# Summing half of the GAT batches on VectorE inside PSUM, slot by slot, in place of pairwise sums of slots

## The chip, the core and the metric

The kernel runs on one core of one Trainium2 chip. The metric is the device time of one launch in microseconds (us). The five engines of the core (TensorE or PE for matmuls, VectorE or DVE, ScalarE or ACT, GpSimd or POOL, SyncE or SP) run their own instruction queues in order and meet through semaphores.

## What is computed

Four graph layers run over 2048 nodes with 8 batches of 128 features. The adjacency matrix is sparse (each entry is 1 with chance 1/128), and it is the same for all batches and layers. Layers 0 and 1 are attention layers with a feed-forward part. Layers 2 and 3 are graph attention (GAT) layers, and only these are touched here:

```python
h = x @ W
e = leaky_relu((h @ a_src)[:, :, None] + (h @ a_dst)[:, None, :], 0.2)
e = where(adj == 0, -inf, e)
out = softmax(e) @ h          # per node: a weighted sum of the rows h of its neighbours
y = layer_norm(out + x)
```

## The kernel before

The 2048 nodes are sorted by their number of neighbours and cut into 16 tiles of 128. A tile of 128 nodes needs as many "slots" as its busiest node has neighbours (`CAPS`, 30 down to 11, 277 slots in all). For each slot one indirect DMA (`gather`, line 320), issued by GpSimd, brings the table row of one neighbour for each of the 128 nodes: in a GAT layer 8 batches x 128 values of `h` and 2 x 8 exponentials, 4160 bytes per node. Slots come in chunks of up to four (`pieces`): a GAT layer has 75 chunks, 53 of four slots, 21 of three, and one "folded" chunk of two slots that serves the 16 busiest nodes. Six buffers hold chunks (`bufs`), and gathers are issued up to five chunks ahead (`fetch`).

The program is written out by hand: `layers` walks over the chunks and calls the steps of each chunk (`go`), which are generators. Between the steps `slot` lets the tails of finished tiles advance (`tails`, `threads`). What stands earlier in the program stands earlier in its engine's queue. The framework adds the semaphore waits for every tile that two engines touch.

The steps of one GAT chunk (`gat_chunk`, lines 728 to 776) are:

- Line 745 to 751, DVE: weights of this chunk's slots and batches, into `pair`, which lies in PSUM, and for the last two batches also into `ws` in SBUF.
- Line 757, DVE: batches 0 to 5 of all slots are multiplied by their weights, in place; one operand is in SBUF and one (`pair`) in PSUM. Line 762, ACT: batches 6 and 7 are multiplied by `ws`, one instruction of 128 values for each slot and batch.
- Line 766, DVE: slots are summed in pairs, over all 8 batches: both operands are in SBUF.
- Line 772, PE: the one or two sums that are left are added into `acc`, a PSUM tile of two banks (batches 0 to 3 and 4 to 7), by matmuls with the identity.

The first two steps of chunk c and the last two of chunk c-1 stand in the same turn of the loop, so line 766 of a chunk follows line 757 of the next one. After the last chunk of a tile, `sums` (line 455) and `outputs` (line 649) divide by the weights' sum, and `gat_tail` adds the residual on PE, normalises (`normed`: ACT squares at line 471, `rs` by GpSimd at line 476, ACT scaling at line 480), and in layer 2 projects the result into the next layer's table, which GpSimd writes by an indirect DMA (line 494). In layer 3 it multiplies and adds on DVE (lines 807, 808) and writes the output (line 810). A layer can start in earnest only when the table of the layer before is complete; a few chunks whose neighbours come early are put ahead (`ORDER`, `EARLY`).

Of the kernel before, what the change touches and what calls it, by code (L numbers as in the profile page):

```python
# [17 lines left out]
P = 128  # L18
# [10 lines left out]
NB = 8  # L29
CHUNK = 4 * NB * (D + 2)  # L30
KVB = 6
SCALED = 2


# [48 lines left out]
def sparse_path(ctx: ExitStack, tc: tile.TileContext, ins: dict, out: bass.AP, flag: bass.AP):  # L83
# [19 lines left out]
    def misc():  # L103
        return pm.tile([P, 512], F32, tag="m", name="m")
# [623 lines left out]
    def gat_chunk(l, c):  # L728
        box, t, k, ns = c["box"], c["t"], c["k"], c["ns"]
        mine = own[:, t, :]  # L730
        if c["folded"]:
            pf = misc()[:, :NB]
            nc.tensor.matmul(pf, spread, mine, start=True, stop=True)
            mine = small.tile([P, NB], F32, tag="mine", name="mine", bufs=1)
            nc.scalar.copy(mine, pf)
            yield
        if k == 0:
            box["acc"] = pacc.tile([P, NB // 4, 512], F32, tag="acc", name="acc")
            at, n = (0 if t % 2 == 0 else 512 - NB * CAPS[t]), CAPS[t]
# [5 lines left out]
        nc.vector.tensor_mul(wb, wb, mine[:, None, :].to_broadcast([P, ns, NB]))  # L745
        nc.vector.tensor_max(wc, wa, wb)
        if c["folded"]:
            box["wf"] = small.tile([P, FOLD, NB], F32, tag="wf", name="wf", bufs=1)
            nc.vector.tensor_max(box["wf"], wa, wb)
        ws = small.tile([P, 4, SCALED], F32, tag="ws", name="ws", bufs=3)  # L750
        nc.vector.tensor_max(  # L751
            ws[:, :ns, :], wa[:, :, NB - SCALED :], wb[:, :, NB - SCALED :]
        )
        yield
        hv = hs[:, :, : NB * D].rearrange("p s (b c) -> p s b c", b=NB)
        nv = NB - SCALED
        nc.vector.tensor_mul(  # L757
            hv[:, :, :nv, :], hv[:, :, :nv, :], wc[:, :, :nv, None].to_broadcast([P, ns, nv, D])
        )
        for i in range(ns):  # L760
            for b in range(nv, NB):
                nc.scalar.mul(hv[:, i, b, :], hv[:, i, b, :], ws[:, i, b - nv : b - nv + 1])  # L762
        yield
        left = -(-ns // 2)
        if ns > 1:
            nc.vector.tensor_add(hv[:, : ns - left], hv[:, : ns - left], hv[:, left:ns])  # L766
        yield
        if c["folded"]:
            folded_sums(box["wf"], box)
        for i in range(left):  # L770
            for j in range(NB // 4):
                nc.tensor.matmul(  # L772
                    acc[:, j, :], merge if c["folded"] else ident, hv[:, i, 4 * j : 4 * j + 4, :],
                    start=k + i == 0, stop=c["last"] and i == left - 1,
                )
        yield

    def gat_tail(l, t, box, i):
# [242 lines left out]
    for l in range(4):  # L1021
        per = 2 if l < 2 else 4
        for t, k, ns, folded in pieces(l, per):
# [2 lines left out]
            c["run"] = (attention_chunk if l < 2 else gat_chunk)(l, c)  # L1026
            every.append(c)
    now = [0, 0]

    def advance(group):  # L1030
        for g in list(group):
# [3 lines left out]
    def fetch():  # L1035

        while now[1] < len(every):
            c = every[now[1]]
            l, t, k, ns = c["l"], c["t"], c["k"], c["ns"]

            if now[1] - now[0] > (4 if now[1] >= KVB and every[now[1] - KVB]["l"] > 1 else 3):
                return
            resorted = l > 0 and t < 2 and not c["folded"]
            need = NT - max([b for end, b in EARLY[t] if k + ns <= end] + [0] if resorted else [0])
            if put[l] < need:
                return
            c["buf"] = buffer()[:, : ns * width(l)].rearrange("p (s c) -> p s c", s=ns)
            for i in range(ns):
                at = t * BASE if resorted else first[t]
                index = (sorted_lists if resorted else lists)[:, at + k + i : at + k + i + 1]  # L1050
                gather(l, index, c["buf"][:, i])
            now[1] += 1

    def slot():
        advance(threads)
        advance(tails)
        fetch()

    def drain():
        while threads or tails:  # L1060
# [3 lines left out]
    def later(n, make):  # L1064
        for _ in range(n):
            yield
        yield from make()
# [30 lines left out]
    def layers():  # L1098
        threads.append(find_lists(0))
        state(0, 0)  # L1100
        drain()
        fetch()
        begin(every[0])
        drain()
        threads.append(find_lists(1))
        for i in range(len(every) + 2):
            now[0] = i
            fetch()
            c2, c1, c, n1, n2 = (chunk(i + j) for j in range(-2, 3))
            if c["k"] == 0:  # L1110
                l, t = c["l"], c["t"]
                if l == 0:
                    if t + 2 < NT:
                        threads.append(find_lists(t + 2))
                    if t == 0:
                        state(0, 1)
                        threads.append(later(12, lambda: state(0, 2) or iter(())))
                        threads.append(later(12, clear_late))
                    if t in (2, 6):
                        threads.append(order_lists(t // 4))  # L1120
                while l < 2 and "asked" not in c["box"]:
# [14 lines left out]
            if c1["l"] in (2, 3) and c1["last"]:  # L1136
                sums(c1["l"], c1["t"], c1["box"])
            go(c)
            slot()
            go(c)  # L1140
            slot()
            if c1["l"] in (0, 1) and c1["last"]:
                sums(c1["l"], c1["t"], c1["box"])
            go(c1, 2)
            if c1["l"] in (2, 3) and c1["last"]:
                threads.append(tail(c1["l"], c1["t"], c1["box"]))
            slot()
        verdict()
        drain()
# [529 lines left out]
```

## Time and profile before

| | |
|---|---|
| time | 3421.26 us, median of 3 runs (3419.2 to 3423.05) |
| span in the profile | 3419.3 us |
| busy, share of the span | DVE 90%, PE 80%, POOL 65%, PE weight loads 46%, ACT 42% |
| mean granted clock of TensorE | 0.917 |
| layers 0 and 1 and the preparation | up to about 2235 us |
| first DVE instruction of layer 2; of its folded chunk | 2234.9; 2335.8 us |
| first DVE instruction of layer 3; of its folded chunk | 2799.7; 2877.9 us |
| last DVE sum of slots; end | 3381.5; 3419.3 us |

The landmarks are starts of DVE instructions in the timeline. Between the first instruction of a GAT layer and its folded chunk, seven early chunks run and the core waits for the end of the layer before. The long stretch from the folded chunk on, with the other 67 chunks, is called the main part below: 463.9 us in layer 2 and 503.6 us in layer 3. In the profile, a group's duration is that of one instruction from its start to its last write; instructions that follow each other overlap at their ends, so the distance from start to start in the timeline is what an instruction costs its engine.

### The profile page before, as it was taken

To read this page: it belongs to the slowest core of one execution; us is meant where nothing else is said; L and a number is where in the kernel's file an instruction comes from. 1 tells how busy PE (TensorE), PEld (TensorE's weight loads), DVE (VectorE), ACT (ScalarE), POOL (GpSimd) and SP (SyncE) were. 2 spreads that over 40 slices of the span, in tenths; PEclk is the share of its full clock that TensorE was granted. 3 is DMA by queue.
4 is the path that set the end of the run, shared out by engine and by line. 5 is a ranking of instruction groups with operands and counts; after the bars stand their busy time and mean duration, and the time that the engine had idled before them with its cause. 6 is when DMAs were issued, how large, how long until landed. Compare 5 with 4: busy or idle time off the path is not lost.

```text
span 3419.3 us, 34694 instructions
## 1 busy us (share of the span) xinstructions
PE 2746.3 (80%) x10618; PEld 1585.2 (46%) x10618; DVE 3063.5 (90%) x2727; ACT 1429.0 (42%) x4972; POOL 2213.2 (65%) x1501
## 2 busy tenths in 40 slices
PE   5647888888989997788888999985888976667775
PEld 4523445445555653455545555642444543233332
DVE  7789999999999989999999999965888876788885
ACT  5711333334444541233334344443555654344444
POOL 0065788688667655465676756646788865688873
PEclk9878999999999999999999999987999997889888
DMA  8487877888888777687887887757999986789883
GB/s 340 181 333 266 300 284 282 314 299 291 307 305 311 279 265 285 229 328 282 318 323 291 300 307 277 283 184 267 334 337 349 346 307 241 276 296 319 297 286 123
DMA packets 200881, 986.52 MB, mean 289 GB/s; under 512 B 32174, under 2 KB 33968, under 8 KB 128692
## 3 DMA queue, kind: packets, MB, share of 16 engines
q0 software_dynamic: 175280, 890.45, 71.8%
q1 hardware_dynamic: 20502, 75.52, 5.7%
q10 hardware_dynamic: 4904, 18.24, 1.4%
q8 instruction: 87, 1.43, 0.2%
q14 instruction: 108, 0.88, 0.1%
HBM read 937.16 MB, written 91.55 MB: 301 GB/s over the span
## 4 chain that ended last, share of the span: by engine, by line
DVE 34%; PE 23%; issue 18%; DMA 10%; POOL 6%; ACT 3%; POOLq 0%; DVEq 0%; ACTq 0%
DVE kv L620 12%; DVE kv L606 12%; PE acc L630 7%; PE acc L772 6%; DMA kv<-table,lists 5%; POOL kv L320 4%; DVE sc L609 2%; DVE kv L757 2%; DMA kv<-table,sorted_lists 2%; DVE kv L766 2%; PE m L712 2%; DVE sums L455 1%; DMA table<-rows,perm 1%; PE m L329 1%; PE m L691 1%
## 5 line engine op out<-in xcount | busy, mean ns | idle before, releaser
L320 POOL DMA_INDIRECT kv<-table,lists x955 | 1422.8, 1490 | 352.6 <-issue 205.8
L630 PE MATMUL acc<-kv,ident 128*128 128x512 f32 x2200 | 1107.2, 633 | 229.4 <-DVE kv L620 229.2
L772 PE MATMUL acc<-kv,ident 128*128 128x512 f32 x1184 | 618.2, 672 | 203.0 <-DVE kv L766 155.6
L630 PEld LDWEIGHTS acc<-kv,ident 128*128 128x128 f32 x2200 | 413.9, 202 | 663.1 <-issue 367.5
L606 DVE TENSOR_TENSOR kv<-kv,q 128x2048 f32<-128x2048 f32 (+1 forms) x282 | 629.4, 2232 | 18.9 <-DMA kv<-table,lists 10.1
L609 DVE TENSOR_REDUCE sc<-kv 128x128 f32<-128x2048 f32 (+1 forms) x284 | 634.0, 2233 | 9.2
L620 DVE TENSOR_TENSOR kv<-kv,w 128x2048 f32<-128x2048 f32 (+1 forms) x284 | 631.5, 2224 | 8.2 <-ACT w L615 7.4
L476 POOL TENSOR_TENSOR rs<-ss,half 128x4 f32<-128x4 f32 x192 | 290.5, 1513 | 422.6 <-ACT n L471 421.1
L471 ACT ACTIVATE n<-m,eps 128x128 f32<-128x128 f32 x768 | 271.9, 367 | 568.7 <-PE m L712 216.7
L772 PEld LDWEIGHTS acc<-kv,ident 128*128 128x128 f32 x1184 | 243.4, 216 | 508.2 <-issue 299.4
L757 DVE TENSOR_TENSOR kv<-kv,pair 128x3072 f32<-128x3072 f32 (+1 forms) x150 | 466.3, 3108 | 1.0
L766 DVE TENSOR_TENSOR kv<-kv 128x2048 f32<-128x2048 f32 (+1 forms) x150 | 296.2, 1975 | 147.3 <-ACT kv L762 147.3
L762 ACT ACTIVATE kv<-kv,ws 128x128 f32<-128x128 f32 x1108 | 339.4, 406 | 146.3 <-DVE ws L751 118.9
L480 ACT ACTIVATE n<-m,rs 128x128 f32<-128x128 f32 x768 | 219.6, 370 | 371.5 <-POOL rs L476 371.2
L615 ACT ACTIVATE w<-sc,lmask 128x64 f32<-128x64 f32 x554 | 164.9, 351 | 457.6 <-DVE sc L609 457.0
L320 POOL DMA_INDIRECT kv<-table,sorted_lists x153 | 199.9, 1307 | 114.5 <-PE acc L630 47.6
L494 POOL DMA_INDIRECT table<-rows,perm x57 | 106.5, 1868 | 110.2 <-ACT rows L518 26.4
L329 PE MATMUL m<-ident,n 128*128 128x128 f32 x640 | 106.9, 289 | 85.3 <-ACT n L480 85.3
L471 ACT ACTIVATION_READ_ACCUMULATOR n<-m,eps 128x1 f32 x768 | 157.4, 205 | 0.0
L712 PE MATMUL m<-w_L_w,hT 128*128 128x128 f32 x1024 | 156.4, 275 | 0.0
L329 PEld LDWEIGHTS m<-ident,n 128*128 128x128 f32 x640 | 81.5, 146 | 142.2 <-ACT n L480 92.7
L712 PEld LDWEIGHTS m<-w_L_w,hT 128*128 128x128 f32 x1024 | 135.2, 192 | 0.0
(234 smaller groups left out, 3237.8 us busy)
## 6 DMA issues: line engine op xcount, KB each, us to landing
kept<-xT SPq DMA_DIRECT2D x48, 512.0 KB, 7.6
xT<-kept SPq DMA_DIRECT2D x48, 512.0 KB, 6.4
kv<-in_adj_dram SPq DMA_DIRECT2D x16, 1024.0 KB, 6.4
table<-kv ACTq DMA_DIRECT2D x16, 1024.0 KB, 4.3
kv<-table,lists POOLq DMA_INDIRECT x955, 7.0
kv<-in_x_nodes_dram SPq DMA_DIRECT2D x16, 512.0 KB, 6.6
kv<-table,sorted_lists POOLq DMA_INDIRECT x153, 6.2
found<-cand POOLq DMA_DIRECT2D x16, 64.0 KB, 4.1
```

What stands on the lines that cost most here:

```text
L320: nc.gpsimd.indirect_dma_start(out=dst, out_offset=None, in_=tables[l][:, :], in_offset=bass.IndirectOffsetOnAxis(ap=index, axis=0), bound ...
L471: nc.scalar.activation(dst[:, i, :], z[:, i, :], AF.Square, bias=eps, scale=D**-0.5, accum_out=ss[:, i : i + 1],)
L476: nc.gpsimd.tensor_tensor(rs, ss, half, op=ALU.pow)
L606: nc.vector.tensor_mul(kk, kk, q[:, None].to_broadcast([P, ns, NB, D]))
L609: nc.vector.tensor_reduce(sc[:, :ns].rearrange("p s (b h) -> p (s b) h", h=NH), kk.rearrange("p s b (h j) -> p (s b) h j", h=NH), axis=AX. ...
L620: nc.vector.tensor_mul(vv, vv, w[:, k : k + ns, :].rearrange("p s (b h) -> p (s b) h", h=NH)[:, :, None, :] .to_broadcast([P, ns * NB, HD, ...
L630: nc.tensor.matmul(acc[:, j, :], merge if c["folded"] else ident, kv[:, i, 4 * j : 4 * j + 4, D:], start=k + i == 0, stop=c["last"] and i ...
L712: nc.tensor.matmul(y[:, j, :], hT[:, f, j, :], wt["2"][:, f, :], start=False, stop=f == 1, skip_group_check=True,)
L757: nc.vector.tensor_mul(hv[:, :, :nv, :], hv[:, :, :nv, :], wc[:, :, :nv, None].to_broadcast([P, ns, nv, D]))
L762: nc.scalar.mul(hv[:, i, b, :], hv[:, i, b, :], ws[:, i, b - nv : b - nv + 1])
L766: nc.vector.tensor_add(hv[:, : ns - left], hv[:, : ns - left], hv[:, left:ns])
L772: nc.tensor.matmul(acc[:, j, :], merge if c["folded"] else ident, hv[:, i, 4 * j : 4 * j + 4, :], start=k + i == 0, stop=c["last"] and i = ...
```

## The change

Batches 0 to 3 no longer go through a product in SBUF, a sum of slots and a matmul. For each slot and each of these four batches one DVE instruction multiplies 128 values by the weight and adds them to the first bank of `acc` (the first slot of a tile only multiplies). The product of line 757 covers only batches 4 and 5, the pairwise sum is gone, and the matmuls add every slot's batches 4 to 7 into the second bank. The weights `ws` are now kept in SBUF for all 8 batches. In the folded chunk the old way stays for the products; its first four batches go through a scratch bank and a copy, and are added to `acc` by one DVE instruction (`add`).

It is meant to take the sum of slots off DVE and, with it, DVE's wait for ACT. Two edits go along: `layers` calls the new third step of a GAT chunk in that chunk's own turn, and `slot` lets the tails advance a second time in every third call (`hurry`) while a GAT layer waits for its table or layer 2 is at its last tile.

```diff
+BANK = 4
 SCALED = 2
...
         nc.vector.tensor_max(wc, wa, wb)
+        ws = small.tile([P, 4, NB], F32, tag="ws", name="ws", bufs=3)
+        nc.vector.tensor_max(ws[:, :ns, :], wa, wb)
+        yield
+        hv = hs[:, :, : NB * D].rearrange("p s (b c) -> p s b c", b=NB)
+        lo, hi = (0 if c["folded"] else BANK), NB - SCALED
+        nc.vector.tensor_mul(
+            hv[:, :, lo:hi, :], hv[:, :, lo:hi, :],
+            wc[:, :, lo:hi, None].to_broadcast([P, ns, hi - lo, D]),
+        )
+        for i in range(ns):
+            for b in range(hi, NB):
+                nc.scalar.mul(hv[:, i, b, :], hv[:, i, b, :], ws[:, i, b : b + 1])
+        yield
+        for i in range(0 if c["folded"] else ns):
+            for b in range(BANK):
+                to, of = acc[:, 0, b * D : (b + 1) * D], ws[:, i, b : b + 1]
+                if k + i == 0:
+                    nc.vector.tensor_scalar_mul(to, hv[:, i, b, :], of)
+                else:
+                    nc.vector.scalar_tensor_tensor(
+                        to, hv[:, i, b, :], of, to, op0=ALU.mult, op1=ALU.add
+                    )
+        yield
...
-        left = -(-ns // 2)
-        if ns > 1:
-            nc.vector.tensor_add(hv[:, : ns - left], hv[:, : ns - left], hv[:, left:ns])
-        yield
...
-        for i in range(left):
-            for j in range(NB // 4):
-                nc.tensor.matmul(
-                    acc[:, j, :], merge if c["folded"] else ident, hv[:, i, 4 * j : 4 * j + 4, :],
-                    start=k + i == 0, stop=c["last"] and i == left - 1,
-                )
+        for i in range(ns):
+            nc.tensor.matmul(
+                acc[:, 1, :], merge if c["folded"] else ident, hv[:, i, BANK:, :],
+                start=k + i == 0, stop=c["last"] and i == ns - 1,
+            )
         yield
...
+    def hurry():
+
+        c = every[min(now[0], len(every) - 1)]
+        return c["l"] == 2 and c["t"] == NT - 1 or c["l"] > 1 and put[c["l"]] < NT
+
     def slot():
         advance(threads)
         advance(tails)
         fetch()
+        beat[0] += 1
+        if beat[0] % 3 == 0 and hurry():
+            advance(tails)
...
             go(c)
             slot()
+            if c["l"] in (2, 3):
+                go(c)
```

More of the change, by code (lines that the diff above doesn't have):

```diff
@@ L746, in gat_chunk @@
         nc.vector.tensor_max(wc, wa, wb)
[L747 to L752, printed above, removed]
-        )
+        ws = small.tile([P, 4, NB], F32, tag="ws", name="ws", bufs=3)
+        nc.vector.tensor_max(ws[:, :ns, :], wa, wb)
@@ L754, in gat_chunk @@
         yield
         hv = hs[:, :, : NB * D].rearrange("p s (b c) -> p s b c", b=NB)
-        nv = NB - SCALED
+        lo, hi = (0 if c["folded"] else BANK), NB - SCALED
         nc.vector.tensor_mul(
-            hv[:, :, :nv, :], hv[:, :, :nv, :], wc[:, :, :nv, None].to_broadcast([P, ns, nv, D])
+            hv[:, :, lo:hi, :], hv[:, :, lo:hi, :],
+            wc[:, :, lo:hi, None].to_broadcast([P, ns, hi - lo, D]),
         )
         for i in range(ns):
-            for b in range(nv, NB):
-                nc.scalar.mul(hv[:, i, b, :], hv[:, i, b, :], ws[:, i, b - nv : b - nv + 1])
+            for b in range(hi, NB):
+                nc.scalar.mul(hv[:, i, b, :], hv[:, i, b, :], ws[:, i, b : b + 1])
@@ L767, in gat_chunk @@
         yield
         if c["folded"]:
-            folded_sums(box["wf"], box)
-        for i in range(left):
-            for j in range(NB // 4):
-                nc.tensor.matmul(
-                    acc[:, j, :], merge if c["folded"] else ident, hv[:, i, 4 * j : 4 * j + 4, :],
-                    start=k + i == 0, stop=c["last"] and i == left - 1,
-                )
+            folded_sums(ws, box)
+            pf = misc()
+            for i in range(ns):
+                nc.tensor.matmul(pf, merge, hv[:, i, :BANK, :], start=i == 0, stop=i == ns - 1)
@@ new lines, in gat_chunk, with add @@
+            merged = work.tile([P, 4, P], F32, tag="oT", name="merged")
+            merged = merged.rearrange("p b c -> p (b c)")
+            nc.scalar.copy(merged, pf)
+            def add():
+                nc.vector.tensor_add(acc[:, 0, :], acc[:, 0, :], merged)
+                yield
+            threads.append(later(4, add))
+        for i in range(ns):
[3 more added lines that the diff above has]
+            )
@@ L1028, in sparse_path @@
     now = [0, 0]
+    beat = [0]
     def advance(group):
```

## The prediction

> **What bounds the kernel now.** Only layers 2 and 3 change, so I read those stages: first the busy time by stage, then the waits of DVE there, then DVE and POOL side by side. The table by stage (columns: stretch, length, then busy us and instructions of PE, PEld, DVE, ACT, POOL, granted clock, DMA share, GB/s; the rows from folded chunk to the layer's end are the main parts):
>
> ```profile
> 2234.90:2335.80 100.90, 68.41 (x319) 43.53 (x318) 44.06 (x42) 45.73 (x171) 40.19 (x39) 0.83 0.50 174
> 2335.80:2799.70 463.90, 386.98 (x1454) 217.06 (x1454) 391.97 (x421) 254.24 (x998) 370.07 (x297) 0.93 0.94 339
> 2799.70:2877.90 78.20, 50.83 (x206) 30.15 (x206) 41.92 (x38) 33.03 (x134) 33.14 (x30) 0.83 0.56 202
> 2877.90:3381.50 503.60, 353.22 (x859) 159.55 (x860) 426.73 (x477) 223.78 (x847) 380.88 (x300) 0.86 0.84 289
> ```
>
> No engine is busy all the time: DVE 392 of 464 us and 427 of 504. The waits of DVE over both layers say where its rest goes:
>
> ```profile
> DVE kv L766 <- ACT kv L762: 147.3, 52, 10.0
> DVE kv L745 <- DMA kv<-table,lists: 46.0, 2, 33.5
> DVE kv L745 <- DMA kv<-table,sorted_lists: 26.9, 9, 11.1
> ```
>
> The two DMA lines are the starts of the layers; inside the main parts gathered rows are hardly waited for (2.8 and 2.9 us). So the pairwise sum waits for ACT's products. ACT in turn waits 277.3 us in these layers at line 480 for `rs` on POOL. And POOL? A gather has a gap of 0.30 us behind it, so its engine is taken 370 + about 0.3 x 270, which is nearly the whole 464 us. It should not be: the shortest gather takes 0.99 us, the mean 1.22 to 1.27. The timelines of POOL and DVE at the same moment show why:
>
> ```profile
> 3172.14 0.99 POOL L320 DMA_INDIRECT kv<-table,lists  x1 [0.31 <-issue]
> 3173.44 2.79 POOL L320 DMA_INDIRECT kv<-table,lists  x1 [0.30 <-issue]
> 3176.54 0.99 POOL L320 DMA_INDIRECT kv<-table,lists  x1 [0.30 <-DMA kv<-table,lists]
> ```
>
> ```profile
> 3169.81 3.35 DVE L757 TENSOR_TENSOR kv<-kv,pair 128x3072 f32<-128x3072 f32 x1
> 3173.08 2.29 DVE L766 TENSOR_TENSOR kv<-kv 128x2048 f32<-128x2048 f32 x1
> 3175.28 0.18 DVE L745 TENSOR_TENSOR kv<-kv,own 128x32 f32<-128x32 f32 x1
> ```
>
> The gather that starts during line 766 ends with it (3176.2 against 3175.4); those during line 757 stay at 0.99. So the bound is a loop: the sum blocks POOL, POOL is late with `rs`, ACT is late, and the next sum waits for ACT.
>
> [...] line 757 starts 3.27 us before its successor, 3.20 us of elements plus 0.07, with an operand in PSUM; line 649 reads `acc` and costs 1.14 us for 1024, also 0.07. [...] DVE and PE will work in different banks of `acc`; no run of before shows whether they can do so here.
>
> **Part by part, DVE.** A cost from start to start is 1.04 us per 1000 elements plus 0.07. The price to find is that of the new instruction, 128 elements and a weight read per partition. Line 432 is the same operation on one element:
>
> ```profile
> 603.25 0.22 DVE L432 SCALAR_TENSOR_TENSOR over<-top,late,over 128x1 f32<-128x1 f32 x1
> 603.38 0.17 DVE L437 CAST sorted_lists<-top 128x28 int32<-128x28 f32 x1
> ```
>
> 0.13 us from start to start, twice the fixed part of an ordinary one. So a new instruction costs 0.133 + 0.133 = 0.266 us. [...] lower bound with a fixed part of 0.07: 0.20. I take 0.266, as PSUM operands cost nothing extra above.
>
> - Chunk of four: removed, line 766 (2.20) and two thirds of line 757 (2048 elements, 2.13), 4.33 us. Added: 16 x 0.266 = 4.26. Before 5.92 us (3169.36 to 3175.28), after 5.87: weights 0.48, product 1.13, sums 4.26.
> - Chunk of three: removed, 1024 and 1536 elements, 2.74 us; added 12 x 0.266 = 3.19. Before 4.06, after 4.50.
> - Main part of a layer: 46 x 5.87 + 21 x 4.50 + 2 for the folded chunk + 16 ends of tiles at 0.75 (line 455 and on) and 1.14 (line 649) = 397 us; before by the same sum 389, measured busy 392. Layer 3 adds lines 807 and 808, 32 x 1.32 = 42: 439.
>
> DVE's work is thus the same. Instead of one long instruction it has 16 short ones.
>
> **The wait that goes and the wait that comes.** Line 766's wait for ACT goes: 57.2 us in the main part of layer 2, 69.0 in layer 3. But the listing of the changed program with its semaphores shows a new pair: the first new sum of chunk c waits for the last `acc` matmul of chunk c-2, and the matmuls of chunk c-1 wait for the last new sum of chunk c. The framework orders DVE and PE on `acc` as one tile, though they use different banks. From the third chunk of a tile on they take turns. Four matmuls are 8 passes of 0.43 us at full clock, 3.42 us; at layer 2's clock of 0.93, 3.67. With 0.25 for the last one's end and the semaphore and 0.14 for DVE's end, DVE is free again after 4.06 us, and has 1.61 us of the next chunk's weights and product to do meanwhile: 2.45 us idle, and 1.83 behind three slots. Of 67 chunks 39 are third or later in their tile: 39 x 2.25 = 88, less the 16 lines 649 that fall into such gaps (18): 70 us. Layer 3, clock 0.86: 39 x 2.5 = 98, less 18, less some 17 of lines 807 and 808 that fall there: 63. Queued behind the waiting DVE instruction are the next chunk's weights, for which ACT and then PE wait.
>
> - Layer 2: 397 + 70 + 3 (rows) = 470 against 464, **+6**.
> - Layer 3: 439 + 63 = 502 against 504, **-2**.
>
> **POOL, DMA, PE.** POOL without blocking needs 256 x 1.30 + 28 x 1.25 + 13 x 1.35 = 386 us in layer 2: freed by nearly 80 us, but hidden behind the 470. DMA moved 157 MB at 0.94 share; at full share it needs 436 us, hidden too. PE loses one of four matmuls in chunks of three, off the path; its tail matmuls (about 2.5 us a chunk) fit under the 4.26 us of sums. The wider `ws`, the folded chunk's copy and `add` are a few us, and lie in the wait for rows at the start: nothing.
>
> **`hurry`.** At the starts of the layers the last tile's tail is the chain: line 643 at 2256.8, its table row write at 2322.5, 66 us, of which some 20 lie after the seventh early chunk's end (2302). A tail takes some 26 turns of `slot`; a third more advances spare it 6. I take 12 us in layer 2, and 8 in layer 3, where the tail is shorter and DVE waits 12.5 us for the folded chunk. Bounds: 0 and 35 together.
>
> Sum: 3421 + 6 - 2 - 20 = 3405; with 2 us for coupling, **3407 us**.
>
> **Rivals.**
> 1. The turns are hidden (PE is done when DVE comes, or the waits are not as strict as listed): then layer 2 stands at DMA's 436 us and layer 3 at DVE's 439, so 3421 - 28 - 65 - 20 = 3308. For it: POOL is free and ACT is off DVE's path. A price of 0.20 for the new instruction (65 us less in each layer) ends near it too, for DMA stops it. Against: PE has 3.4 us of matmuls for 1.6 us of other DVE work, and line 432 shows the dearer price. Chance 0.12.
> 2. [...] For it: no row of before reads and writes PSUM in one instruction. Chance 0.13.
> 3. ACT's lateness returns through PE: the matmuls need ACT's products, and PE's queue holds tail transposes that wait for line 480. If half of the 126 us comes back: 3470. Against: POOL is no longer late, and a chunk of slack lies between. Chance 0.15.
> 4. The turns as I have them, but no gain at the starts: 3427. Chance 0.10.
>
> My own forecast has 0.50, with some 25 us to each side for the clock and the lengths of the gaps.
>
> **How the numbers follow.** Faster: rival 1 and about seven tenths of my case, 0.49; same: the parts of my case and of rival 4 around 3421, 0.11; slower: rivals 2, 3, half of 4 and the rest, 0.40. The range, 3340 to 3490, leaves out most of rivals 1 and 2.
>
> **What would show it.** Right: no gather over 1.5 us outside lines 807 and 808; DVE sums start to start at 0.27 us; a DVE wait for `acc` matmuls of 110 to 160 us in place of 147 for ACT; main parts within 15 us of 464 and 504; starts shorter by 20. Wrong: [...] DVE waiting for PE below 60 or above 220 us, or rows waited for in the main parts.

## The result, and the profile after

The changed kernel takes **3779.4 us** (median of 4 runs, 3776.1 to 3782.4) against 3422.2 us for the kernel before: ratio **1.104**, 95% interval 1.102 to 1.106. It is slower by 357 us. The forecast of 3407 us has the wrong sign, and the time lies far outside its range.

Lines have moved: 745 is now 748, 757 is 755, the new sums are 767 (first slot of a tile) and 769, the matmuls on `acc` 788 (772 before), `add` 783, `outputs` 652 (649), the gathers 323 (320), lines 807 and 808 are 823 and 824, the ACT scaling of `normed` 483 (480). The table by stage of the changed kernel, with the same columns as before (stretch, length, busy us and instructions of PE, PEld, DVE, ACT, POOL, granted clock, DMA share, GB/s): start of layer 2, its main part, start of layer 3, its main part.

```profile
2230.70:2326.30 95.60, 69.55 (x328) 44.35 (x326) 54.86 (x148) 45.21 (x171) 39.00 (x38) 0.91 0.53 178
2326.30:2982.90 656.60, 453.52 (x1429) 239.78 (x1430) 477.87 (x1342) 267.78 (x1012) 302.42 (x301) 0.80 0.72 245
2982.90:3051.10 68.20, 56.14 (x193) 32.12 (x191) 51.56 (x142) 30.38 (x121) 25.39 (x25) 0.82 0.54 186
3051.10:3734.90 683.80, 386.09 (x812) 172.22 (x811) 512.34 (x1391) 227.48 (x844) 304.33 (x299) 0.75 0.63 213
```

Against before the starts are 5 and 10 us shorter, the main parts 193 and 180 us longer. POOL is relieved, as was meant (302 busy us against 370), and the rows are far from the limit (DMA share 0.72 against 0.94). PE has fewer matmuls in layer 2's main part (1429 against 1454), yet is busy for longer (454 us against 387), at a clock of 0.80 in place of 0.93. The waits of DVE (in all, times, longest):

```profile
DVE acc L769 <- PE acc L788: 262.2, 71, 5.5
```

That is the wait for `acc` that was forecast, at twice its size. The timeline of one turn, all engines (start, length, engine, line; in brackets the idle time before and what ended it; lines of POOL and some of DVE left out):

```profile
3616.07 6.22 DVE L769 SCALAR_TENSOR_TENSOR acc<-kv,ws,acc 128x128 f32<-128x128 f32 x16
...
3622.20 1.22 DVE L652 TENSOR_TENSOR o<-acc,sums 128x1024 f32<-128x1024 f32 x1
...
3622.55 5.31 PE L788 MATMUL acc<-kv,ident 128*128 128x512 f32 x8 [10.59 <-DVE acc L769]
...
3624.39 0.33 PEld L788 LDWEIGHTS acc<-kv,ident 128*128 128x128 f32 x1 [0.52 <-issue]
...
3625.24 0.33 PEld L788 LDWEIGHTS acc<-kv,ident 128*128 128x128 f32 x1 [0.52 <-issue]
3625.98 0.19 PEld L788 LDWEIGHTS acc<-kv,ident 128*128 128x128 f32 x1 [0.41 <-issue]
3626.41 0.19 PEld L788 LDWEIGHTS acc<-kv,ident 128*128 128x128 f32 x1 [0.24 <-issue]
...
3627.90 4.66 DVE L769 SCALAR_TENSOR_TENSOR acc<-kv,ws,acc 128x128 f32<-128x128 f32 x12 [1.82 <-PE acc L788]
```

Two things are to be seen. First, 16 sums take 6.22 us. From the first sum to line 652, which follows at 3622.20, it is 6.13 / 16 = **0.383 us** each, not 0.266, although one lasts only 0.356 us (group of line 769: mean 356 ns): each starts just after the one before has ended. Second, PE comes out of 10.59 us of idleness, and its eight passes take **5.31 us** where eight that follow other work without a pause take 3.67 (a line further below). This turn is no exception: over all groups of eight passes that stand together, the mean is 5.5 us in the main part of layer 2 and 5.8 us in that of layer 3. The weight loads give the pace of the passes: 0.85 us apart at first (3624.39 to 3625.24), 0.43 us at the end (3625.98 to 3626.41).

So the theory is: (i) every sum waits for the end of the one before, because the framework orders all accesses to one PSUM bank of a tile, whatever the place within it; (ii) DVE and PE take turns on `acc`, as predicted; (iii) the turns leave PE idle, and its first passes then run at half speed. Rivals: the instruction is dear in PSUM by itself; `hurry` or the order of steps causes the loss; ACT's lateness, not the turns, holds DVE; the clock is low over the whole stage for a reason of its own.

### The profile page after: what moved, and what is told of

Same layout as the page of the kernel before. It is cut to its first block, busy times and chain, and to the rows that moved or that the text cites. A ratio compares the mean times of both kernels' runs of the same rounds, so it can differ in the third digit from the quotient of the medians.

```text
span 3774.3 us, 37113 instructions
## 1 busy us (share of the span) xinstructions
PE 2853.8 (76%) x10542; PEld 1625.1 (43%) x10542; DVE 3256.0 (86%) x4777; ACT 1444.1 (38%) x4974; POOL 2068.7 (55%) x1501
## 4 chain that ended last, share of the span: by engine, by line
DVE 41%; PE 27%; issue 16%; DMA 5%; ACT 3%; POOL 2%; POOLq 0%; DVEq 0%; ACTq 0%
PE acc L788 12%; DVE kv L623 11%; DVE kv L609 11%; DVE acc L769 10%; PE acc L633 6%; DVE sc L612 2%; DMA kv<-table,lists 2%; ACT n L474 2%; DVE kv L755 2%; PE m L715 1%; DVE sums L458 1%; DMA kv<-table,sorted_lists 1%; PE m L694 1%; POOL kv L323 1%; DVE acc L767 1%
## 5 line engine op out<-in xcount | busy, mean ns | idle before, releaser
L323 POOL DMA_INDIRECT kv<-table,lists x955 | 1314.0, 1376 | 732.9 <-PE acc L788 328.8
L633 PE MATMUL acc<-kv,ident 128*128 128x512 f32 x2200 | 1108.7, 634 | 221.2 <-DVE kv L623 221.0
L788 PE MATMUL acc<-kv,ident 128*128 128x512 f32 x1100 | 712.1, 809 | 480.5 <-issue 173.5
L769 DVE SCALAR_TENSOR_TENSOR acc<-kv,ws,acc 128x128 f32<-128x128 f32 x2072 | 737.2, 356 | 332.0 <-PE acc L788 262.2
L633 PEld LDWEIGHTS acc<-kv,ident 128*128 128x128 f32 x2200 | 413.6, 202 | 653.9 <-issue 368.2
L788 PEld LDWEIGHTS acc<-kv,ident 128*128 128x128 f32 x1100 | 274.9, 262 | 844.9 <-issue 618.0
L323 POOL DMA_INDIRECT kv<-table,sorted_lists x153 | 184.5, 1206 | 119.4 <-PE acc L633 40.5
L755 DVE TENSOR_TENSOR kv<-kv,pair 128x1024 f32<-128x1024 f32 (+1 forms) x150 | 172.9, 1153 | 0.0
L497 POOL DMA_INDIRECT table<-rows,perm x57 | 89.9, 1577 | 141.9 <-ACT rows L548 40.5
L694 PE MATMUL m<-n1T,w_L_gnn_W 128*128 128x512 f32 x256 | 130.6, 593 | 0.4 <-ACT n L483 0.4
L332 PE MATMUL m<-ident,n 128*128 128x128 f32 x640 | 98.9, 278 | 25.5 <-ACT n L483 25.5
```

Source lines behind the costliest of these rows:

```text
L323: nc.gpsimd.indirect_dma_start(out=dst, out_offset=None, in_=tables[l][:, :], in_offset=bass.IndirectOffsetOnAxis(ap=index, axis=0), bound ...
L633: nc.tensor.matmul(acc[:, j, :], merge if c["folded"] else ident, kv[:, i, 4 * j : 4 * j + 4, D:], start=k + i == 0, stop=c["last"] and i ...
L755: nc.vector.tensor_mul(hv[:, :, lo:hi, :], hv[:, :, lo:hi, :], wc[:, :, lo:hi, None].to_broadcast([P, ns, hi - lo, D]),)
L769: nc.vector.scalar_tensor_tensor(to, hv[:, i, b, :], of, to, op0=ALU.mult, op1=ALU.add)
L788: nc.tensor.matmul(acc[:, 1, :], merge if c["folded"] else ident, hv[:, i, BANK:, :], start=k + i == 0, stop=c["last"] and i == ns - 1,)
```

## The experiments

### The price of one sum

A kernel that holds nothing but eight rows of 64 DVE operations, 128 elements each, between marker copies: sums on four places of one PSUM bank (as in the changed kernel), on four banks in turn, on two banks in turn, a product with a weight per partition in SBUF, sums in SBUF on four places, sums in SBUF on one place, plain additions over four banks, plain additions on four places of one bank.

```diff
+for i in range(64): scalar_tensor_tensor(**mac(bank[0][:, i % 4 * D : i % 4 * D + D], i))   # line 38
+for i in range(64): scalar_tensor_tensor(**mac(bank[i % 4][:, :D], i))                      # 41
+for i in range(64): scalar_tensor_tensor(**mac(bank[i % 2][:, :D], i))                      # 44
+for i in range(64): tensor_scalar_mul(near[:, i % 4, :], hv[:, i % 16, :], weight)          # 47
+for i in range(64): scalar_tensor_tensor(**mac(near[:, i % 4, :], i))                       # 50
+for i in range(64): scalar_tensor_tensor(**mac(near[:, 0, :], i))                           # 53
+for i in range(64): tensor_add(bank[i % 4][:, :D], bank[i % 4][:, :D], hv[:, i % 16, :])    # 56
+for i in range(64): tensor_add(...)  # line 59, as 56, on four places of bank[0]
```

> This kernel leaves the whole computation out and only measures prices: rows of 64 DVE operations on 128 elements with nothing beside them. Theory (each new sum waits for the end of the one before it, because the framework orders all writers of one PSUM bank): the multiply-and-add on four places of one bank, as in the changed kernel, takes 0.38 us from start to start; on four tiles in four banks, or two banks in turn, 0.27; in SBUF on four places 0.27; in SBUF always on the same place 0.38. Rival (reading and writing PSUM in one instruction is dear by itself): 0.33 to 0.38 in all PSUM forms, banks or not, and 0.27 in SBUF in both forms. The product with a pointer weight alone, SBUF to SBUF: 0.27 if the pointer doubles the fixed part, 0.20 if not; the plain sum of two operands 0.20 over four banks.

DVE's timeline of it:

```profile
6.27 24.94 DVE L38 SCALAR_TENSOR_TENSOR bank<-hv,ws,bank 128x128 f32<-128x128 f32 x64
31.12 0.22 DVE L39 COPY o<-hv 128x128 f32<-128x128 f32 x1
31.25 16.62 DVE L41 SCALAR_TENSOR_TENSOR bank<-hv,ws,bank 128x128 f32<-128x128 f32 x64
47.79 0.22 DVE L42 COPY o<-hv 128x128 f32<-128x128 f32 x1
47.92 16.62 DVE L44 SCALAR_TENSOR_TENSOR bank<-hv,ws,bank 128x128 f32<-128x128 f32 x64
64.46 0.22 DVE L45 COPY o<-hv 128x128 f32<-128x128 f32 x1
64.59 12.61 DVE L47 TENSOR_SCALAR near<-hv,ws 128x128 f32<-128x128 f32 x64
77.13 0.21 DVE L48 COPY o<-hv 128x128 f32<-128x128 f32 x1
77.27 16.87 DVE L50 SCALAR_TENSOR_TENSOR near<-hv,ws,near 128x128 f32<-128x128 f32 x64
94.07 0.21 DVE L51 COPY o<-hv 128x128 f32<-128x128 f32 x1
94.20 24.75 DVE L53 SCALAR_TENSOR_TENSOR near<-hv,ws,near 128x128 f32<-128x128 f32 x64
118.87 0.22 DVE L54 COPY o<-hv 128x128 f32<-128x128 f32 x1
```

From the start of a row to its marker, over 64: one bank (31.12 - 6.27) / 64 = **0.388 us**; four banks and two banks 0.258; SBUF on four places 0.263, on one place 0.385. The price of the instruction is thus 0.26 us, in PSUM as in SBUF, and 0.13 us more are paid whenever it has to wait for the one directly before; at a distance of two the wait is gone. Rival "dear in PSUM" falls. The additions over four banks (line 56, 119.00 to 131.67) cost 12.67 / 64 = 0.198 us, those on four places of one bank (line 59, 131.80 to 153.12) 0.333: the wait costs them as much. The dearer fixed part (0.258 - 0.133 = 0.125 us, against 0.065 for the addition) thus belongs to the multiply-and-add, as the prediction's price row had it. The product with a weight costs 12.54 / 64 = 0.196 us; how much of that is the weight, one size can't tell.

That the order comes from the program can be read in its listing: of the 2072 sums of line 769, 1956 wait for DVE's own semaphore to reach the value that the instruction directly before sets. With the sums in SBUF (below) the same wait mostly reaches back four instructions, with two banks in turn two.

### acc as two tiles: no turns

```diff
-    box["acc"] = pacc.tile([P, NB // 4, 512], F32, tag="acc", name="acc")
+    box["acc"] = [pacc.tile([P, 512], F32, tag=f"acc{j}", name=f"acc{j}") for j in range(2)]
...
-    to, of = acc[:, 0, b * D : (b + 1) * D], ws[:, i, b : b + 1]
+    to, of = acc[0][:, b * D : (b + 1) * D], ws[:, i, b : b + 1]
...
-        acc[:, 1, :], merge if c["folded"] else ident, hv[:, i, BANK:, :],
+        acc[1], merge if c["folded"] else ident, hv[:, i, BANK:, :],
```

> acc becomes two tiles of one bank, so that DVE's sums and PE's matmuls are no longer ordered on one tile; each sum still waits for the one before. Theory (turns and the wait of each sum on the one before are two separate losses): DVE's wait for acc matmuls falls from 262 us to under 20, sums stay at 0.38 us, main parts 656 - 132 = 524 and 684 - 125 = 559, time 3779 - 257 = 3522. Rival 1 (DVE is slow for a reason outside the turns, and would wait for ACT's or PE's other results in their place): 3650 to 3780. Rival 2 (two engines in different banks slow each other): sums above 0.40 us, matmuls no shorter, 3600 or more.

Measured: 3532.8 us (3528.6 to 3535.1), ratio 1.033 (1.031 to 1.035). DVE's largest wait is now 36.8 us for rows at a layer's start; none for acc matmuls is left before the sums. The main parts:

```profile
2327.10:2858.60 531.50, 392.38 (x1444) 223.05 (x1445) 476.42 (x1356) 259.89 (x1012) 301.95 (x301) 0.86 0.85 303
2925.90:3497.50 571.60, 333.63 (x821) 159.89 (x822) 510.61 (x1407) 226.19 (x845) 302.48 (x299) 0.79 0.71 254
```

DVE is as busy as in the changed kernel (476 and 511 us), but its idle time falls from 179 and 171 us to 55 and 61. The turns thus cost 3779.4 - 3532.8 = 247 us; no wait for another engine took their place, and working in neighbouring banks at once did neither engine harm: 16 sums still take 6.13 us from start to start (2819.60 to 2825.73), and a pass lasts 592 ns in the median (2612 to 2792 us) where the changed kernel has 849 (2501 to 2699 us). What is new is a small one: some 31 us of stops of about 0.35 or 1.05 us between one sum and the next, which the changed kernel does not have.

### The sums in SBUF, in two orders

The four sums go to a tile `near` in SBUF; there the framework orders by place. In the second kernel the two loops are exchanged, so that each sum follows the one on its own place.

```diff
+    box["near"] = work.tile([P, max(CAPS), NB * NH], F32, tag="w", name="near")
...
-    to, of = acc[:, 0, b * D : (b + 1) * D], ws[:, i, b : b + 1]
+    to, of = near[:, b * D : (b + 1) * D], ws[:, i, b : b + 1]
```

```diff
-        for i in range(0 if c["folded"] else ns):
-            for b in range(BANK):
+        for b in range(BANK):
+            for i in range(0 if c["folded"] else ns):
```

> The four sums are held in SBUF in place of PSUM; acc keeps the other four batches. The built program orders sums in SBUF by place, so each waits for the one four back, and DVE and PE share no tile. Theory: sums at 0.27 us, no wait for acc matmuls, DVE busy or waiting for rows: main parts near 440 and 445, time about 3320 to 3340, if the sums' two SBUF inputs do not hold back GpSimd's gathers; if they do as the pairwise sum did (gathers of 1.2 us and more), 3340 to 3420. Rival (the instruction is dear wherever it works): sums 0.36 us or more, time above 3480.

> As the kernel with the sums in SBUF, only the two loops exchanged: all slots of one batch follow one another, so that 13 sums of 16 wait for the one directly before. Theory: these 13 take 0.38 us from start to start, 800 x 0.117 = 94 us more DVE time in each layer, so 120 to 190 us longer than with the loops as they were. Rival (the wait for the instruction before costs nothing, the place PSUM does): within 15 us of the other order.

Measured: 3425.1 us (3409.4 to 3436.2), ratio 1.001 (1.000 to 1.002), so no change from before; and 3482.2 us in chains, 1.019 (1.017 to 1.021), 57 us more. The main parts with the sums in SBUF, first order:

```profile
2331.10:2801.80 470.70, 373.14 (x1410) 211.32 (x1411) 389.39 (x1356) 252.56 (x994) 369.98 (x297) 0.89 0.93 335
2883.30:3386.00 502.70, 314.18 (x805) 144.17 (x804) 425.24 (x1407) 216.78 (x825) 378.35 (x299) 0.82 0.84 289
```

These are nearly the main parts of before (463.9 and 503.6), with POOL at 370 and 378 busy us, as before (370 and 381). Both losses of the changed kernel are gone, and its gain with them: with both inputs of the sums in SBUF, gathers are held again (mean 1257 ns in layer 2 against 1004 in the changed kernel). In layer 2's main part the 134 gathers that begin beside a sum take 1.5 us in the mean and up to 3.7, the other 121 take 1.0. So the second half of the expectation came about, just above its upper end. In chains DVE's busy time rises by 64 and 57 us in the main parts, and the time by 30 and 35: 57 us in all, where 120 to 190 were expected. DVE was not the bound in the first order, and POOL is down to 310 us, its gathers at 1038 ns: between sums that wait for each other they get through. In the first order most held gathers of layer 2 (44 of 60) end 0.86 or 1.46 us after the last sum of the row, much as they did after line 766 (0.86 us); about as many begin under such a row and are not held, and why, no run shows.

### Two PSUM banks in turn: neither turns nor waits

Built on the kernel with two tiles. The sums of batches 0 and 1 lie in one bank and those of 2 and 3 in another; the order 0, 2, 1, 3 puts two sums on one bank two instructions apart. To make room in PSUM both banks are single: the first half of `outputs` moves into `sums`, where only DVE's own work is needed, and tile 0, which overlaps with tile 1, keeps its sums in SBUF.

```diff
+    two = [pacc.tile([P, 512], F32, name=f"near{x}", tag=x, bufs=1) for x in "ab"]
+    box["near"] = [two[b // 2][:, b % 2 * D : b % 2 * D + D] for b in range(BANK)]
...
-    for b in range(BANK):
-        to, of = acc[0][:, b * D : (b + 1) * D], ws[:, i, b : b + 1]
+    for b in (0, 2, 1, 3):
+        to, of = near[b], ws[:, i, b : b + 1]
```

> Two changes to the kernel with two acc tiles: the four sums lie in two PSUM banks (batches 0 and 1 in one, 2 and 3 in the other) and are taken in the order 0, 2, 1, 3, so that each waits for the one two back; to make room the first half of the outputs is written as soon as a tile's sums are done. Only tile 0 keeps its sums in SBUF. Theory: sums at 0.26 us as in the price kernel, gathers stay at 1.0 us because the sums still have one operand in PSUM; DVE's work falls by 988 x 0.125 = 123 us in each main part, to 408 and 448; in layer 2 the rows then set the time (436 us at full DMA share). Main parts 440 to 455 and 450 to 465, time 3533 - 85 - 115 = 3333, between 3310 and 3360, so faster than before. Rival (ACT's or PE's lateness comes back in place of DVE's, as with the sums in SBUF): 3400 to 3440. Rival (PSUM sums are dear while PE works in other banks): 3500 or more.

Measured: **3291.7 us** (3290.6 to 3293.8), ratio **0.9625** (0.961 to 0.964): 3.75% faster than before, and 41 us better than expected. This is the version that beats both kernels. Its main parts:

```profile
2331.80:2740.30 408.50, 358.25 (x1412) 204.72 (x1413) 389.07 (x1374) 252.60 (x998) 304.21 (x296) 0.94 0.99 386
2816.00:3258.40 442.40, 322.23 (x835) 147.26 (x835) 422.28 (x1420) 222.06 (x841) 309.36 (x298) 0.88 0.90 329
```

DVE is busy for 389 and 422 us, POOL for 304 and 309. In layer 2 two things are close to full at once: between its waits DVE fills 393 of 408 us, and the DMA share is 0.99, though DVE waits only 4 us for rows in the main part. The 436 us that the prediction and this expectation took as DMA's floor were no floor: 339 GB/s at a share of 0.94 made 361 at full share, but here 386 GB/s pass at 0.99. Against the kernel with sums in SBUF, where the number of sums is the same and their pace nearly so, the gathers' mean in layer 2 is 1002 ns in place of 1257. The two differ also in where the first half of `outputs` is written, so not all of the 133 us between them need be the gathers'.

### The turns put back by themselves

A matmul of 2x2 elements before and after a chunk's acc matmuls writes an unused corner of the first of the two banks. This restores the order between DVE and PE, at the price of these small matmuls (0.19 us a pair in the timeline).

```diff
+        left = CAPS[t] - (k + ns) if t > 0 else 0
+        if left > 0:
+            mark = box["two"][0][:2, 2 * D : 2 * D + 2]
+            nc.tensor.matmul(mark, ident[:, :2], ident[:, :2], start=True, stop=True)
         for i in range(ns):
             nc.tensor.matmul(far, ...)
+        if left > 4:
+            nc.tensor.matmul(mark, ident[:, :2], ident[:, :2], start=True, stop=True)
```

> The kernel with two banks taken in turn, with the turns put back: before and after the acc matmuls of a chunk a matmul of 2x2 elements writes an unused corner of the first of the two banks, so that DVE and PE are ordered there as they were on acc (not for tile 0 and not after a tile's last two chunks). Sums keep their 0.26 us. Theory a (a turn costs what the prediction took, eight passes at 0.43 us): main parts near 470 and 502 as predicted, 3292 + 120 = 3412. Theory b (in a turn PE comes out of an idle stretch and its first passes take twice as long, 1.7 us more for each of some 36 turns and layer): 3292 + 120 + 120 = 3530; between them if the shorter sums leave PE less time to idle. Rival (turns cost little when sums are at 0.26 us): below 3340.

Measured: 3482.1 us (3480.7 to 3487.9), ratio 1.018 (1.016 to 1.021). DVE waits 225 us for the marks:

```profile
DVE neara L797 <- PE neara L825: 225.0, 70, 13.6
```

The time lies between the two theories: the main parts are 508.0 and 536.1 us, 38 and 34 above the 470 and 502 of the prediction's turns. Sums at the predicted price do not make the turns as cheap as predicted. With the kernels above this gives a square of times:

| | sums do not wait for each other | each sum waits for the one before |
|---|---|---|
| no turns | 3292 | 3533 (+241) |
| turns | 3482 (+190) | 3779 (+487) |

The two losses account for 431 of the 487 us; 56 come only with both. The split is not sharp: the left column also writes half of the outputs earlier and keeps tile 0's sums in SBUF, and 3533 holds the 31 us of short stops that the other three kernels do not have. Where 56 us can come from is visible: groups of eight passes take 4.6 and 5.0 us in the mean in the two main parts here, and 5.5 and 5.8 in the changed kernel (a single pass lasts 712 ns here and 818 there, in the mean from 2340 to 3690 us). The next experiments look at why.

### Cold passes

A kernel with groups of ten matmuls (20 passes of 512 columns) and idle stretches of growing length ahead of them.

```diff
+for us in (0, 0.5, 1, 1.5, 2, 3, 4, 6, 10, 0, 1, 2, 3, 4):
+    tensor_copy(seen, bank[:, :1]); memset(idle[:, : int(us * 1160)], 0.5); memset(ticket[:, :64], 0.5)
+    matmul(bank[:, :64], ident, ticket[:, :64])          # waits for the ticket
+    for i in range(10): matmul(bank, ident, hv)
```

> This kernel leaves the whole computation out: groups of ten fp32 matmuls of 512 columns (20 passes) on PE, with idle stretches between the groups that a DVE memset of growing length sets (about 0.4, 0.9, 1.4, 1.9, 2.4, 3.4, 4.4, 6.4 and 10.4 us, then 0.4, 1.4, 2.4, 3.4 and 4.4 again). Theory: after idle stretches up to some limit below 3 us every pass takes 0.43 us (a group 8.5 us); after longer ones the first four or five passes take 0.85 us, so the group 1.7 to 2.1 us longer, and no more after 10 us than after 4. Rival (the granted clock falls over a whole stage): the groups stay at one length, whatever the stretch ahead.

PE's timeline; line 39 is the first matmul after the stretch, with the stretch in brackets, line 41 the group:

```profile
44.36 0.43 PE L39 MATMUL bank<-ticket,ident 128*128 128x64 f32 x2 [2.14 <-DVE ticket L38]
44.63 8.80 PE L41 MATMUL bank<-hv,ident 128*128 128x512 f32 x20
56.18 0.49 PE L39 MATMUL bank<-ticket,ident 128*128 128x64 f32 x2 [2.75 <-DVE ticket L38]
56.47 10.48 PE L41 MATMUL bank<-hv,ident 128*128 128x512 f32 x20
70.91 0.69 PE L39 MATMUL bank<-ticket,ident 128*128 128x64 f32 x2 [3.96 <-DVE ticket L38]
71.39 11.55 PE L41 MATMUL bank<-hv,ident 128*128 128x512 f32 x20
...
130.80 0.69 PE L39 MATMUL bank<-ticket,ident 128*128 128x64 f32 x2 [12.42 <-DVE ticket L38]
131.28 10.62 PE L41 MATMUL bank<-hv,ident 128*128 128x512 f32 x20
```

After 2.14 us of idleness a group takes 8.80 us, as it does after every shorter one; from 2.75 us on it takes 10.2 to 11.6 us, and 12.4 us of idleness are no worse than 4. The penalty is 1.4 to 2.8 us, and the turn of the changed kernel (5.31 us against 3.67) pays 1.6. In this kernel the limit lies between 2.14 and 2.75 us.

In the changed kernel itself, PE was kept at work by further matmuls on ones after each chunk's acc matmuls: 20 in the first kernel, 6 in layer 2 and 14 in layer 3 in the second.

```diff
+        warm = misc().rearrange("p (b c) -> p b c", c=D)
+        for i in range(20):                      # second kernel: range(6 if l == 2 else 14)
+            nc.tensor.matmul(
+                warm, ones_bf, ones_bf[:, None, :].to_broadcast([P, 4, D]), start=True, stop=True
+            )
```

> The changed kernel, with 20 further matmuls of bf16 ones (0.21 us each at full clock) into a misc bank after the acc matmuls of every chunk; their result is not read. They fill the time in which PE waits for DVE's sums. Theory (in each turn the first four or five passes run at half speed because PE comes out of a long idle stretch): the eight passes of a turn take 3.5 to 3.9 us in place of 5.3, DVE's wait for acc matmuls falls from 262 us to 140 to 170, time 3779 - 105 = 3670, between 3640 and 3700, although PE has more to do. Rival (the passes are long because the throttle grants less clock over the whole stage): the eight passes stay at 5 us or more, time 3770 to 3850.

> As the kernel with 20 further matmuls, with 6 of them in layer 2 and 14 in layer 3, because 20 filled PE in layer 2 (631 of 648 us busy) and held the acc matmuls back. Theory (cold passes make a turn 1.7 us longer): DVE's wait for acc matmuls 150 to 180 us in all in place of 227, time 3680 to 3720. Rival (the length of the passes does not set DVE's wait): 3750 or more.

Measured: 3750.4 us (3743.3 to 3752.9), ratio 1.096 (1.094 to 1.098), and 3696.4 us (3688.6 to 3705.2), 1.081 (1.077 to 1.084). In a turn of the first kernel that PE enters without an idle stretch (timeline):

```profile
3464.62 3.67 PE L788 MATMUL acc<-kv,ident 128*128 128x512 f32 x8
```

DVE's wait for acc matmuls, first and second kernel:

```profile
DVE acc L769 <- PE acc L788: 227.1, 68, 9.2
```

```profile
DVE acc L769 <- PE acc L788: 179.4, 71, 6.4
```

In the first kernel PE has more work, and its eight passes take 3.67 us in place of 5.31, in the mean of layer 2's groups too. In the second, with fewer further matmuls, DVE's wait falls by 83 us and so does the time, which lies where it was expected (3680 to 3720). The granted clock of the main parts is 0.99 and 0.97 in the first kernel, where PE idles little, against 0.80 and 0.75 in the changed one. So the clock is low because PE idles, and cold passes make up a good part of DVE's wait; the rest is the turn itself. The first kernel missed its mark (105 us expected, 29 measured): its extra matmuls filled PE in layer 2 (631 of 647.5 us busy), so the acc matmuls came late there. In layer 3, where there was room, the wait fell from 125.0 to 83.7 us. The kernel before also shows that length of idleness alone does not decide; two groups of its layer 3:

```profile
3123.34 3.70 PE L772 MATMUL acc<-kv,ident 128*128 128x512 f32 x8 [3.36 <-DVE kv L766]
...
3168.41 5.37 PE L772 MATMUL acc<-kv,ident 128*128 128x512 f32 x8 [1.97 <-issue]
```

Eight passes took 3.70 us after 3.36 us of idleness and 5.37 us after 1.97. What else decides, no run here shows.

### hurry alone, and without it

```diff
+        beat[0] += 1
+        if beat[0] % 3 == 0 and hurry():
+            advance(tails)
```

added to the kernel before, and the last two of these lines taken out of the changed one.

> The kernel before with hurry alone: a third more advances of the tails at the starts of layers 2 and 3. Theory (hurry is a small gain of its own): the starts 5 and 10 us shorter, nothing else moves, 3421 - 15 = 3406. Rival (hurry or its turns cost elsewhere): 3421 or more.

> The changed kernel without hurry. Theory: the starts 5 and 10 us longer, nothing else moves, 3779 + 15 = 3794. Rival (hurry causes part of the loss): below 3770.

Measured: 3419.2 us (3414.8 to 3426.8), ratio 0.9995 (0.9985 to 1.0006), and 3786.0 us (3781.0 to 3790.9), ratio 1.107 (1.104 to 1.109) against 1.104 (1.102 to 1.106) with it. Neither is a difference that can be told from none. In the kernel before, the starts do become shorter (97.5 and 72.7 us against 100.9 and 78.2), but the main parts become longer by 8 and 4 us; POOL is busy there for as long as before (374 and 384 us). `hurry` is no cause of the loss. Nor is the order of the steps: the kernel with two banks in turn keeps it and is the fastest.

### A batch more on ACT

In the kernel with two banks in turn DVE is busy for 422 of 442 us of layer 3; there a third batch is multiplied by ACT.

```diff
-        lo, hi = (0 if c["folded"] else BANK), NB - SCALED
+        lo, hi = (0 if c["folded"] else BANK), NB - (SCALED if l == 2 else 3)
```

> The kernel with two banks taken in turn, with a third batch multiplied by ACT in place of DVE in layer 3 (layer 2 as it was, since the rows set its time at 0.99 DMA share). In layer 3 DVE is busy 422 of 442 us. Theory (DVE sets layer 3): 247 slots x 128 elements leave DVE, 247 x 0.133 = 33 us, of which DMA (442 x 0.90 = 398 us at full share) lets nearly all count: main part 415, time 3292 - 27 = 3265. Rival (ACT's products are already what PE and the rows wait for in layer 3, 168 us of PE's load wait and 12 of DVE's): 3290 or more.

Measured: 3374.8 us (3367.8 to 3378.6), ratio 0.9855 (0.984 to 0.987): 83 us slower than without the edit. DVE's busy time in layer 3 fell to 398 us, by 24 of the 33 us worked out, but the main part grew to 477.7 us: DVE now stands idle for 80 us of it in place of 20. Some 50 of these are short stops between sums, with no other engine behind them; the largest of DVE's waits for itself, from 2750 us on:

```profile
DVE neara L797 <- DVE nearb L797: 16.7, 30, 1.1
DVE nearb L797 <- DVE neara L797: 12.7, 24, 1.1
```

They are of about 0.35 or 1.05 us, as in the kernel with two tiles; the kernel with two banks in turn has none. Layer 2, whose instructions were not touched, took 446.2 us in place of 408.5, with DVE idle for 55 us in place of 19, 15 of them in such stops. The theory missed. The rival had the direction but not the reason: PE's wait for ACT's products at its acc matmuls in layer 3 fell from 103.0 to 86.6 us. What causes the stops stays open.

## Why the prediction was wrong, step by step

- **The bound of before: right.** The loop of line 766, POOL, `rs` and ACT is what held the main parts. The sums in SBUF bring POOL's 370 us and the times of before back; with an operand in PSUM POOL falls to 302 to 309 us, and the best kernel gains 3.75%. In the changed kernel no gather of chunks in the main parts reaches 1.5 us (the longest take 1.063 and 1.499), and DVE no longer waits for ACT's products, as foreseen. The prediction's reading that the held gather ends with line 766 is loose: it ends 0.86 us after it (3176.23 against 3175.37), where a gather that is not held takes 0.99 us in all, so by that estimate nearly all its work comes then.
- **The new instruction at 0.266 us: right as a price, wrong as a distance from start to start.** Measured alone it is 0.258 us in PSUM and 0.263 in SBUF, close to the forecast and above its lower bound of 0.20. The step that failed is "988 x 0.266": the sums stand in a row on one bank, and each waits for the end of the one before. 0.383 - 0.266 = 0.117 us more, times 988, is **116 us in each main part** that the sum did not have. The prediction read the listing for the waits between DVE and PE and put the wait of each sum on DVE's own semaphore at nothing, without a reason; four instructions back, as in SBUF (0.263 us), it would have been free. The price row, line 432, was followed by an instruction that did not depend on it, so it could not show this.
- **DVE's work "the same": wrong by that term.** Between its waits DVE fills 514 of 657 us and 550 of 684 in the main parts (busy for 478 and 512 us; the rest are gaps too short to be counted as waits, most between one sum and the next), where 397 and 439 were worked out.
- **The turns: right in kind and number, too short.** 71 waits on `acc` came, 35 in each main part where 39 were counted, for the instructions named. But they take 132.4 and 125.0 us, not 70 and 63. The term that failed is "3.67 us at layer 2's clock of 0.93": the mean clock of a stage of the kernel before was taken as given, though the turns themselves make PE idle and so halve its pace for the first passes (0.85 us apart in place of 0.43). To the end of the last pass the prediction allowed 3.67 + 0.25 = 3.92 us in layer 2 and, at 0.86, 4.23 in layer 3; the mean groups of eight take 5.5 and 5.8. Some 1.6 us more in each of 35 turns is about 55 us for each layer, of the 62 that are missing; the rest is not taken apart.
- **The sum with these terms at their measured sizes** is 470 + 116 + 62 + 6 (wait of line 783) = 654 us for layer 2, measured 656.6; and 502 + 116 + 62 + 6 = 686 for layer 3, measured 683.8. Both are within 3 us, so no other large term is missing.
- **hurry at 20 us: not shown.** The starts did become 15 us shorter, but the kernel without `hurry` is only 7 us slower, within the uncertainty, and the kernel before gains nothing by it.
- **The rivals.** Rival 1, turns hidden at 3308 us, is near what the kernel without turns and waits does (3292), in part by luck: its layer 2 stood at a DMA floor of 436 us that is none (408.5). Rival 2 named the dear sum, with a wrong reason: a price of PSUM, which no run shows (0.258 us there against 0.263 in SBUF). Rival 3, ACT's lateness coming back through PE, did not come in the changed kernel (DVE waits 11.6 us at line 652 for PE); with the sums in SBUF DVE waits 77.7 us at that place. The range failed because both unknown costs were bounded by prices of single operations, and no bound was put on a wait between them. Its own sign of being wrong, DVE waiting for PE for over 220 us, came (262.2).

## What to carry to other kernels

Before one long instruction is replaced by many short ones, ask for each short one which instruction it waits for and how far back that is: a wait on the direct predecessor costs half as much again as the instruction here (0.388 us from start to start against 0.258), and two banks in turn take it away. Two engines that work on two banks of one tile take turns here (262 us of DVE's waits), and with two tiles they do not; and an engine that idles in a turn may come back slow (eight passes in 5.31 us in place of 3.67), so a clock read from the profile before is not a constant of the stage (0.93 before, 0.80 after in layer 2's main part). A gain in the loop that bounds a kernel can be real and still be buried under the form in which it is written: here the same idea gives +10.4% or -3.75%.

## What the runs showed of the hardware

- A DVE multiply-and-add with a weight per partition on 128 elements costs 0.258 us from start to start, of which 0.125 is a fixed part by an estimate with 1.04 us per 1000 elements (line 757 of the kernel before, start to start: 3.27 us for 3072 elements at 2400.55 us, 2.47 for 2304 at 2406.46); a product with such a weight or a plain addition costs 0.196 to 0.198. PSUM operands add nothing (0.263 us in SBUF). A wait on the instruction just before adds 0.13 us (0.388 in one bank; 0.385 on one place of SBUF).
- PE passes of 512 fp32 columns are 0.43 us apart, and 0.85 us for the first ones after an idle stretch of some length. In a kernel of nothing but such groups 2.14 us of idleness slow none (8.80 us for 20 passes) and 2.75 us do (10.48); in the kernel before eight passes were not slowed after 3.36 us (3.70 us) and slowed after 1.97 (5.37).
- The share of time in which the DMA engines are busy is not a measure of what is left: at 0.94 they moved 339 GB/s, at 0.99 386.
- Gathers issued while DVE runs sums with both inputs in SBUF take 1257 ns in the mean in layer 2, but 1038 where each sum waits for the one before; with one input in PSUM they take 1002 to 1004.
